# Attention with sparsemax on one core: small queries on column tiles, a head loaded from two queues, split relus in the last batch, and a new order

## The chip, the core and the metric

The kernel runs on one core of a Trainium2 chip. The core has a matrix engine (TensorE, PE), which multiplies a stationary block of up to 128x128 by moving columns and writes into PSUM; three engines for elementwise work (VectorE or DVE, ScalarE or ACT, GpSimd or POOL); and SyncE (SP), used here as a queue that issues transfers between main memory and on-chip memory (SBUF). Each engine executes its own instructions in order and waits for the others by semaphores. The metric is the device time of one launch in microseconds (us), as the median of several runs. A profiled execution is one run with a hardware trace.

## The reference

Eight batches of 100 rows with 512 features go through a cross-attention block with 16 heads of 32 features and a two-branch feed-forward block, all in 32-bit floats. The context of each batch has 722 rows.

```python
qh = split_heads(layernorm(x) @ Wq + bq)
kh = split_heads(ctx @ Wk + bk)
vh = split_heads(ctx @ Wv + bv)
scores = einsum('bhqd,bhkd->bhqk', qh, kh) * 32 ** -0.5
attn = sparsemax(scores)              # max(s - tau, 0), tau so that each row sums to 1
x = x + merge_heads(attn @ vh) @ Wo + bo
h = layernorm(x)
real = h @ cos(theta + theta_noise)
imag = h @ sin(phi + phi_noise)
out = x + sqrt(real ** 2 + imag ** 2)
```

Sparsemax needs a threshold tau for each row of scores. It is the fixed point of an iteration over the largest scores of the row.

## The kernel before

**Tiles.** The 800 rows of x are laid end to end and cut into seven token tiles: six of 128 rows and, fourth in order, a small one of 32 rows (`TILES`, with `HD` = 32). Layer norm, queries, output product and feed-forward go by token tile; keys, scores, sparsemax, values and weights go by batch. The context comes transposed, so that a chunk of 128 features lies on the 128 partitions.

**Scores and thresholds.** For each batch the 100 queries of the 16 heads give 13 groups of 128 score rows. Five *fills* (`fill`, L800, L789) write scores into the one large PSUM tile `psc` of four banks, by matmuls with 32 rows of contraction that share the array. ACT copies each fill to SBUF (`fill_copy`, L811), and DVE takes the eight largest of each of 24 segments of a row (`tops`, L822). From these `rests` and `candidates` make a list of 80 candidates in a row. `first_bound` gives a first threshold, and five rounds improve it (`above` on DVE, `above_values` on POOL, `above_count` and `update` on DVE). `losses` (three DVE instructions, L985 to L987) finds the largest score that may have been left out of the list; `keep_checks` on POOL keeps it for a verdict at the end, after which a slower path is taken if the list was too short. `parts` on POOL splits the thresholds into three bf16 parts, `parts_T` transposes them on PE (L951). In the last batch the thresholds are made in three spans of the groups (5, 4 and 4 of them), so that the first are done sooner.

**Weights and outputs.** A second set of matmuls makes the scores again, now transposed and less the threshold (`weights`, L995 and L1008), five pairs of a head group and a context chunk at a time, again in `psc`. A relu with the scale moves them to SBUF (`weights_relu`, L1027 on ACT), and `outputs` (L1042) multiplies them with the values. In the last batch the relus of odd number write into a buffer of the fills (`s_t`), the others into `aT`; the last of the five is cut in two, heads 0 and 1 on ACT (L1027) and heads 2 and 3 on DVE (L1029).

**Queries.** `queries` (L554) makes the four groups of 128 query features one after the other: `Wq` is stationary, the normed rows, transposed, are moving. For the small tile there are 32 moving columns. `small_product` (L580), used for the small tile's other three products, makes the rows stationary instead and writes the four groups of 128 features under each other, 32 partitions each, so that the four column tiles of the array work side by side.

**Head.** DVE fills a bf16 tile with -1, and PE multiplies it with itself `WARM` times (`warm_up`, L512) before the first real work. The first batch's keys are made by chunks of features as these land: `load_pair` issues a chunk of `Wk` (256 KB) and of the context (361 KB) on SP's queue, and `keys_part` (L706) multiplies six pieces (three head groups, two halves of the context).

**Tail.** The last token tile is finished by `last_steps_of_all`: its output product goes in four parts as the head groups come in, its feed-forward in two halves of 352 and 160 columns (`half_ffn`, L638, then `half_square`, `half_sum`, `half_root`, `half_result`), each half with its own store.

**The order.** Every step is a task with an engine, a cost in us (`STEPS`), the tasks it needs, and the buffers it takes (`hold`). `Plan.order` simulates the engines: an engine that is free takes the task that can start first, and among these the one with the earliest due time. The due time comes from the batch (`PERIOD`, `SHIFT`), the longest path to the end, and a table of shifts for each kind of step and batch (`LAG`, `NUDGE`); on PE a task whose use of the array is the same as that of the one before (`SHAPE`: full, 32x32, column tiles, row tiles) counts as `STAY` us earlier. The tasks are then emitted in the order of their simulated starts, and that is the order of the instructions on every engine and queue. `SHAPE` and `CHANGE` also give a cost in the plan for each change of the array's use. `LATENCY` is the plan's delay from one engine to the next.

Of the kernel before, what the change touches and what calls it, by code (L numbers as in the profile page):

```python
# [11 lines left out]
FP = mybir.dt.float32  # L12
# [9 lines left out]
HD = 32  # L22
# [24 lines left out]
def fills_of(left_first):  # L47
# [34 lines left out]
WARM = 32  # L82
# [17 lines left out]
    "load x": ("SP", 0.7),  # L100
# [3 lines left out]
    "load bias": ("SP", 0.1),  # L104
    "load pair": ("SP", 1.9),
    "warm up": ("PE", 2.1),
    "stats": ("DVE", 0.85),
    "deviation": ("ACT", 0.25),
    "normed": ("DVE", 0.72),
# [30 lines left out]
    "values last": ("PE", 2.7),  # L140
# [10 lines left out]
    "small residual": ("DVE", 0.9),  # L151
# [14 lines left out]
    "half result": ("DVE", 0.15, 0.00105),  # L166
    "store": ("SP", 0.6),
# [10 lines left out]
SHAPE = {"fill": 1, "fill last": 2, "outputs": 2, "small product": 2, "values last": 2, "weights": 3}  # L178
CHANGE = (0.19, 0.1, 0.1, 0.1)
STAY = 70.0  # L180

SHIFT = (-195.0, -175.0, -45.0, -130.0, -190.0, -205.0, -190.0, -220.0)
PERIOD = 121.0
WINDOW = 0.0
LAG = {
    "above": -95.0,
    "above count": -140.0,
    "above values": 280.0,
    "add bo": 265.0,
    "bounded": -170.0,  # L190
    "candidates": 295.0,
    "checks": 170.0,
    "deviation": -255.0,
    "ffn": 300.0,
    "fill": -290.0,
    "fill copy": -95.0,
    "fill last": -220.0,
    "first bound": -65.0,
    "half ffn": 230.0,
    "half result": 285.0,  # L200
    "half root": -130.0,
    "half square": -155.0,
    "half sum": -40.0,
    "keys": 115.0,
    "keys bias": 10.0,
    "keys part": -215.0,
    "leftovers": -85.0,
    "load bias": 85.0,
    "load ctx": 215.0,
    "load pair": -270.0,  # L210
    "load w": -80.0,
    "load x": -285.0,
    "load x again": 185.0,
    "losses": 75.0,
    "normed": -200.0,
    "normed 2": -120.0,
    "normed T": -145.0,
    "normed copy": 175.0,
    "output product": -10.0,
    "outputs bias": -85.0,  # L220
    "parts": -75.0,
    "parts T": 160.0,
    "parts copy": -300.0,
    "parts copy last": -200.0,
    "product part": -120.0,
    "queries": -300.0,
    "queries bias": -125.0,
    "relu ACT": 155.0,
    "relu DVE": 300.0,
    "residual": -85.0,  # L230
    "rests": -140.0,
    "result": -210.0,
    "sines": 230.0,
    "small product": -250.0,
    "small residual": -130.0,
    "small root": 55.0,
    "small square": -245.0,
    "small sum": -275.0,
    "square": -240.0,
    "square sum": -10.0,  # L240
    "stats": 290.0,
    "stats 2": 290.0,
    "store": -285.0,
    "tops": 175.0,
    "turned": 175.0,
    "turns": -70.0,
    "update": -85.0,
    "values": 210.0,
    "values copy": -205.0,
    "values last": 260.0,  # L250
    "values last copy": 220.0,
    "verdict": 155.0,
    "verdict T": 220.0,
    "verdict most": 90.0,
    "warm up": -60.0,
    "weights": -110.0,
    "weights relu": 265.0,
# [3 lines left out]
    "deviation": {6: 45.0},  # L261
    "ffn": {2: 150.0, 5: 150.0},
    "fill": {7: 190.0},
    "fill last": {2: -85.0},
    "first bound": {7: 150.0},
    "keys": {1: 10.0, 7: -100.0},
    "load bias": {0: 15.0},
    "load pair": {0: 35.0},
    "load w": {0: 170.0},
    "load x": {0: 50.0, 3: -20.0, 4: -180.0},  # L270
    "normed T": {2: 30.0},
    "output product": {2: 200.0},
    "outputs": {6: 20.0, 7: -25.0},
    "product part": {7: 110.0},
    "values": {0: 5.0, 2: -130.0, 3: -125.0, 5: -20.0, 6: 30.0, 7: 120.0},
    "weights": {1: 105.0, 5: 140.0, 6: 130.0},
# [16 lines left out]
class Plan:  # L293
# [3 lines left out]
    LATENCY = {"PE": 0.25, "SP": 2.0}  # L297
# [43 lines left out]
    def order(self):  # L341
# [8 lines left out]
        while len(done) < len(self.tasks):  # L350
            best = None
            for engine, waiting in ready.items():
                now, pick = free_at[engine], None
                for t in waiting:
                    start = max([now, t.ready] + [self.slot(h["name"]) for h in t.takes])
                    if start < math.inf:
                        stay = STAY if engine == "PE" and t.shape == shape else 0.0
                        key = (max(start, now + WINDOW), t.due - stay)
                        if pick is None or key < pick[0]:
                            pick = (key, start, t)  # L360
# [19 lines left out]
            for n in t.next:  # L380
                late = self.LATENCY.get(t.engine, 0.2)
                n.ready = max(n.ready, t.end + (0.0 if n.engine == t.engine == "SP" else late))
# [7 lines left out]
def xattn_ffn(  # L390
# [55 lines left out]
    def load_x(rows_of_x, n):  # L446

        x_t = rows.tile([P, DM], FP, name="x_t", bufs=3)[:n]
        nc.sync.dma_start(x_t, rows_of_x)
        return x_t  # L450
# [5 lines left out]

    def load_pair(st, b, c):

        if c == 0:
            st["c"] = big.tile([P, NG, S], FP, name="c_t")  # L460
# [126 lines left out]

    def small_residual(tk):
# [72 lines left out]
    def half_result(tk, h):  # L661
        a = tk["sq", 0][:, half_of(h)]
        nc.vector.tensor_tensor(a, a, tk["x"][:, half_of(h)], ALU.add)
# [32 lines left out]
    def keys_part(st, c):  # L696
# [7 lines left out]
        for n in range(EARLY):  # L704
            g, i = divmod(n, 2)
# [370 lines left out]
    def once(fn):  # L1076
        return add("load bias", fn)

    def set_x(tk):
        at, n = tk["at"], tk["n"]  # L1080
        tk["x"] = load_x(x.rearrange("b q d -> (b q) d")[at : at + n], n)
# [27 lines left out]
    def token_steps(tk):  # L1109
# [3 lines left out]
        hold("x", tk["x in"], [h])  # L1113
# [508 lines left out]
```

## Time and profile before

| What | Value |
|---|---|
| Median of three runs | 591.64 us (591.42 to 594.48) |
| Profiled execution, its own time | 594.34 us |
| Its span, first to last instruction | 592.6 us |
| Mean granted clock of PE | 0.995 |
| First matmul of the warm-up | 1.19 us |
| First matmul of the keys | 4.79 us |
| First `tops` on DVE | 30.07 us |
| Last group of half products begins | 585.68 us |
| Last store issued | 588.39 us |
| POOL busy | 224.2 us (38%) |
| Bytes moved by transfers | 26.61 MB |

A row of a profile gives the engine, the line of the kernel, the operation, the tile that is written and what is read, the shape, and the count. A matmul in 32-bit floats is two instructions. Matmuls overlap in the array, so their own durations are longer than the distance from one start to the next. The line of waits names an engine, what it was about to do, and which instruction of which engine ended the wait. A view by stretches gives each engine's busy time between two times, and the share of PE's clock that was granted.

### The profile page before, as it was taken

What the parts mean: (1) busy time and instruction counts of PE and PEld (TensorE: products, weight loads), DVE (VectorE), ACT (ScalarE), POOL (GpSimd) and SP (SyncE); (2) the same over time, 40 slices, a digit from 0 to 9 for tenths busy, and PEclk for the clock granted to TensorE, in tenths of its full rate; (3) what the DMA queues carried; (4) which work ended last, traced back from release to release, by engine and by line L of the source; (5) the groups of instructions that cost most, each with busy time, mean ns of one, the idle gap of its engine ahead of it and who ended that gap; (6) DMA issues with size and microseconds to landing.
All of it is one profiled execution on the core that took longest, in us unless ns stands there. A gap on an engine that the chain in (4) does not pass through costs nothing.

```text
span 592.6 us, 18085 instructions
## 1 busy us (share of the span) xinstructions
PE 580.5 (98%) x6937; PEld 339.1 (57%) x6937; DVE 517.3 (87%) x3186; ACT 261.8 (44%) x399; POOL 224.2 (38%) x293
## 2 busy tenths in 40 slices
PE   9999999999999999999999999999999999999995
PEld 6655554567456743677457744576557544664553
DVE  3299999998999879998999899999999899999521
ACT  1353352455346523654345434363545534552532
POOL 1686799974400232004620232015200446045402
PEclk9999999999999989999999999999999999999999
DMA  8940300310011000200100002030000001000001
GB/s 323 316 136 20 118 19 19 108 49 2 19 35 70 2 1 2 102 3 20 43 2 3 2 2 101 3 102 2 3 2 2 14 25 59 3 20 1 3 2 39
DMA packets 12475, 26.61 MB, mean 45 GB/s; under 512 B 1872, under 2 KB 2128, under 8 KB 12384
## 3 DMA queue, kind: packets, MB, share of 16 engines
q1 hardware_dynamic: 11952, 24.03, 12.4%
q8 instruction: 56, 0.92, 0.6%
q0 software_dynamic: 432, 1.38, 0.6%
q14 instruction: 35, 0.29, 0.2%
HBM read 23.76 MB, written 1.64 MB: 43 GB/s over the span
## 4 chain that ended last, share of the span: by engine, by line
PE 60%; DVE 32%; POOL 4%; ACT 2%; issue 1%; DVEq 0%; POOLq 0%; ACTq 0%
PE pm L717 18%; DVE cand L822 15%; PE pm L738 10%; PE psc L1008 5%; PE pm L612 5%; PE pm L1042 4%; PE psc L800 4%; PE pm L554 3%; DVE f L907 3%; DVE m L889 3%; POOL p L894 2%; DVE n L900 2%; PE pm L754 2%; PE psc L706 2%; PE psc L995 2%; DVE rest L831 1%
## 5 line engine op out<-in xcount | busy, mean ns | idle before, releaser
L822 DVE MAX8 cand<-s_t 128x8 f32<-128x30 f32 x2496 | 230.7, 171 | 1.4 <-ACT s_t L811 1.4
L894 POOL TENSOR_TENSOR p<-z,m 128x1040 f32<-128x1040 f32 (+2 forms) x50 | 88.7, 1778 | 266.7 <-DVE m L889 261.8
L717 PE MATMUL pm<-c_t,wk_sb 128*128 128x361 f32 x464 | 152.5, 474 | 0.0
L738 PE MATMUL pm<-wv_sb,c_t 128*128 128x512 f32 x320 | 144.3, 598 | 0.0
L717 PEld LDWEIGHTS pm<-c_t,wk_sb 128*128 128x128 f32 x464 | 84.1, 189 | 53.8 <-issue 10.8
L738 PEld LDWEIGHTS pm<-wv_sb,c_t 128*128 128x128 f32 x320 | 58.5, 190 | 66.7 <-issue 65.6
L811 ACT COPY s_t<-psc 128x1924 f32<-128x1924 f32 (+2 forms) x40 | 69.1, 1726 | 50.1 <-DVE cand L822 30.0
L1027 ACT ACTIVATE aT<-psc 128x2000 f32<-128x2000 f32 (+2 forms) x38 | 66.5, 1749 | 53.2 <-PE pm L1042 36.2
L767 ACT COPY v_t<-pm 128x512 f32<-128x512 f32 x40 | 23.4, 586 | 85.1 <-PE pm L738 85.1
L907 DVE TENSOR_REDUCE f<-p 128x13 f32<-128x1040 f32 (+2 forms) x50 | 50.4, 1009 | 10.6 <-POOL p L894 10.5
L728 ACT ACTIVATE k_t<-pm,bk_sb 128x361 f32<-128x361 f32 x60 | 33.5, 562 | 55.8 <-PE pm L717 55.7
L900 DVE TENSOR_REDUCE n<-m 128x13 f32<-128x1040 bf16 (+2 forms) x50 | 50.3, 1007 | 0.6
L1008 PE MATMUL psc<-q_t,k_t 32*128 32x100 f32 (+1 forms) x1536 | 47.4, 264 | 0.0
L1008 PEld LDWEIGHTS psc<-q_t,k_t 32*128 32x128 f32 (+1 forms) x1536 | 46.4, 180 | 0.4
L800 PE MATMUL psc<-k_t,q_t 32*32 32x481 f32 (+1 forms) x1536 | 43.3, 474 | 0.8 <-ACT s_t L811 0.7
L1042 PE MATMUL pm<-aT,v_t 128*32 128x100 f32 (+1 forms) x1440 | 39.2, 251 | 0.1
L1042 PEld LDWEIGHTS pm<-aT,v_t 128*32 128x32 f32 (+1 forms) x1440 | 30.9, 109 | 7.1 <-issue 3.3
L554 PEld LDWEIGHTS pm<-hT,wq_sb 128*128 128x128 f32 x224 | 27.1, 191 | 6.3 <-issue 5.4
L554 PE MATMUL pm<-hT,wq_sb 128*128 128x128 f32 (+1 forms) x224 | 29.6, 280 | 0.0
L800 PEld LDWEIGHTS psc<-k_t,q_t 32*32 32x32 f32 x1536 | 14.0, 103 | 26.2 <-issue 19.4
L754 PE MATMUL pm<-wv_sb,c_t 128*18 128x128 f32 (+1 forms) x384 | 23.6, 311 | 0.0
L831 DVE MAX8 rest<-cand 128x8 f32<-128x120 f32 x104 | 20.1, 268 | 0.2
(307 smaller groups left out, 615.6 us busy)
## 6 DMA issues: line engine op xcount, KB each, us to landing
c_t<-in_ctx SPq DMA_DIRECT2D x7, 1444.0 KB, 6.6
x_t<-in_x SPq DMA_DIRECT2D x12, 256.0 KB, 3.1
c_t<-in_ctx SPq DMA_DIRECT2D x4, 361.0 KB, 5.1
out<-sq POOLq DMA_DIRECT2D x5, 256.0 KB, 2.8
wk_sb<-in_L_xattn_Wk SPq DMA_DIRECT2D x4, 256.0 KB, 4.6
wq_sb<-in_L_xattn_Wq SPq DMA_DIRECT2D x4, 256.0 KB, 5.7
cos_sb<-in_L_ffn_theta SPq DMA_DIRECT2D x4, 256.0 KB, 4.5
n_t<-in_L_ffn_theta_noise SPq DMA_DIRECT2D x4, 256.0 KB, 3.1
```

The costliest lines, as they stand in the source:

```text
L554: nc.tensor.matmul(tk["pq"][:, g, : tk["n"]], lhsT=wq_sb[:, c, g * P : (g + 1) * P], rhs=tk["hT"][:, c, :], start=(c == 0), stop=(c == NG ...
L717: nc.tensor.matmul(pk, lhsT=wk_sb[:, c, g * P : (g + 1) * P], rhs=st["c"][:, c, i * SH : (i + 1) * SH], start=(c == 0), stop=(c == NG - 1),)
L738: nc.tensor.matmul(pv, lhsT=st["c"][:, k, c * CK : (c + 1) * CK], rhs=wv_sb[:, k, :], start=(k == 0), stop=(k == NG - 1),)
L800: nc.tensor.matmul(psc[b * HD : (b + 1) * HD, j, at : at + EDGE[hi] - EDGE[lo]], lhsT=st["q"][r, g, qb * HD : (qb + 1) * HD], rhs=st["k"][ ...
L811: nc.scalar.copy(s_t[:, :, :n], st["psc"][:, :, :n])
L822: nc.vector.max(st["cand"][:, n, k, :], st["s", f][:, j, at + EDGE[k] - first : at + EDGE[k + 1] - first],)
L894: nc.gpsimd.tensor_tensor(st["p"][:, lo:hi], st["z"][:, lo:hi], st["m"][:, lo:hi], ALU.mult)
L900: nc.vector.tensor_reduce(n_t, st["m"][:, lo:hi], AX.X, ALU.add)
L907: nc.vector.tensor_reduce(s_t, st["p"][:, lo:hi], AX.X, ALU.add)
L1008: nc.tensor.matmul(psc[:m, j, k * Q : (k + 1) * Q], lhsT=st["k"][r, g, lo : lo + m], rhs=st["q"][r, g, :], start=False, stop=(k == len(PAI ...
L1027: nc.scalar.activation(a, b, AF.Relu, scale=SCALE)
L1042: nc.tensor.matmul(st["po", g][j * HD : (j + 1) * HD, :Q], lhsT=st["v"][:m, c, f : f + HD], rhs=aT[j][:m, j, k * Q : (k + 1) * Q], start=( ...
```

## The change

1. `WARM` goes from 32 to 20.
2. The first chunk of the first batch's keys is loaded in two steps (`load_first`): `Wk`'s first 128 columns and then the other 384 on ACT's queue, the two halves of the context on SP's. `keys_part` goes through the first half of the context for all three head groups and then through the second.
3. The small tile's queries are made by `small_product`, copied from PSUM into the small tile's own buffer of x (`small_copy`, on ACT) and transposed on PE (`small_T`), after which the bias is added as before. The buffer of x is held until the transpose.
4. In the last batch all five relus are cut in two: heads 0 and 1 on ACT, heads 2 and 3 on DVE, with the buffers `aT` and `s_t` changing sides from one to the next.
5. `losses` is put ahead of the last (or only) `first_bound` of a batch, which now waits for it.
6. The second half of the last result is added on POOL instead of DVE.
7. In the plan, tiled work after tiled work of another kind counts as `STAY_TILED` us earlier; some costs and the delay after SP are changed; and the tables of shifts are new, so that the whole program has another order.

```diff
-WARM = 32
+WARM = 20
@@ STEPS
-    "load x": ("SP", 0.7),
+    "load x": ("SP", 0.85),
-    "load bias": ("SP", 0.1),
+    "load bias": ("SP", 0.45),
+    "load bv": ("SP", 0.45),
+    "load bo": ("SP", 0.8),
+    "load first": ("SP", 1.3),
-    "warm up": ("PE", 2.1),
+    "warm up": ("PE", 2.3),
-    "normed": ("DVE", 0.72),
+    "normed": ("DVE", 0.9),
+    "small queries": ("PE", 0.95),
+    "small copy": ("ACT", 0.33),
+    "small T": ("PE", 0.15),
+    "last result": ("POOL", 0.1, 0.0026),
...
-STAY = 70.0
+STAY = 155.0
+STAY_TILED = 140.0
-PERIOD = 121.0
+PERIOD = 147.0
...
-    LATENCY = {"PE": 0.25, "SP": 2.0}
+    LATENCY = {"PE": 0.25, "SP": 2.6}
...
-                        stay = STAY if engine == "PE" and t.shape == shape else 0.0
+                        stay = 0.0
+                        if engine == "PE":
+                            stay = STAY if t.shape == shape else STAY_TILED if t.shape and shape else 0.0
...
-                late = self.LATENCY.get(t.engine, 0.2)
-                n.ready = max(n.ready, t.end + (0.0 if n.engine == t.engine == "SP" else late))
+                late = 0.0 if n.engine == t.engine else self.LATENCY.get(t.engine, 0.2)
+                n.ready = max(n.ready, t.end + late)
...
+    def load_first(st, b):
+        st["c"] = big.tile([P, NG, S], FP, name="c_t")
+        for i in range(2):
+            w_cols = slice(P, DM) if i else slice(0, P)
+            nc.scalar.dma_start(wk_sb[:, 0, w_cols], wk[:P, w_cols])
+            keys_i = slice(i * SH, (i + 1) * SH)
+            nc.sync.dma_start(st["c"][:, 0, keys_i], ctxT[b, :P, keys_i])
...
+    def small_copy(tk):
+        tk["qs"] = tk["x whole"][:, :P]
+        nc.scalar.copy(tk["qs"], tk["pq"])
+    def small_T(tk):
+        pt = ps1.tile([P, NG, P], FP, name="pm")
+        nc.tensor.transpose(pt[:, 0, :], tk["qs"], ident)
+        tk["pq"] = pt[:, 0, :].rearrange("p (g t) -> p g t", g=NG)
...
-    def half_result(tk, h):
+    def half_result(tk, h, engine):
         a = tk["sq", 0][:, half_of(h)]
-        nc.vector.tensor_tensor(a, a, tk["x"][:, half_of(h)], ALU.add)
+        engine.tensor_tensor(a, a, tk["x"][:, half_of(h)], ALU.add)
...
-        for n in range(EARLY):
-            g, i = divmod(n, 2)
+        for i, g in sorted((n % 2, n // 2) for n in range(EARLY)):
...
+        if tk["n"] == HD:
+            pq = add("small queries", lambda: small_product(tk, "pq", "hT", wq_sb), hT, *w["q"])
+            cp = add("small copy", lambda: small_copy(tk), pq)
+            qs = [add("small T", lambda: small_T(tk), cp)]
+            hold("hT", hT_in, [pq])
+            hold("pm", pq, [cp])
+            hold("x", tk["x in"], qs)
...
-            rz = add("half result", lambda h=h: half_result(tk, h), rt, tiles=z - a)
+            rz = add(
+                "last result" if h else "half result",
+                lambda h=h: half_result(tk, h, nc.gpsimd if h else nc.vector), rt, tiles=z - a,
+            )
...
+            if hi == NT:
+                ls = add("losses", lambda st=st: losses(st), *cds, *rest_steps)
+            t = add(
+                "first bound", lambda st=st, r=r: first_bound(st, **r), cd, *([ls] if hi == NT else ()),
+                tiles=hi - lo,
+            )
...
-        ls = add("losses", lambda st=st: losses(st), *cds, *rest_steps)
...
-            if b == B - 1 and n == len(PAIRS) - 1:
+            if b == B - 1:
                 es = [
                     add(
                         "relu ACT" if k else "relu DVE",
                         lambda st=st, n=n, k=k: weights_relu(
-                            st, n, not k, slice(0, 2) if k else slice(2, HG), k
+                            st, n, (n + k) % 2 == 0, slice(0, 2) if k else slice(2, HG), k
                         ),
-                        f, tiles=len(pairs),
+                        f, *top_steps, tiles=len(pairs),
                     )
-                    for k in (True, False)
+                    for k in (1, 0)
                 ]
-                takes = {"aT": es[0], "s": es[1]}
+                takes = {"aT": es[n % 2], "s": es[1 - n % 2]}
```

## The prediction

> **What bounds the kernel now.** I read the busy times first, then the stretches of the run, then the waits of the matrix engine, then the order in time at three places.
>
> ```profile
> PE 580.5 (98%) x6937; PEld 339.1 (57%) x6937; DVE 517.3 (87%) x3186; ACT 261.8 (44%) x399; POOL 224.2 (38%) x293
> ```
>
> TensorE (PE) is in use in all but 12.1 us of the 592.6 us span. The five stretches show where VectorE (DVE) comes close.
>
> ```profile
> 0.00:30.00 30.00, 28.81 (x165) 20.07 (x166) 8.65 (x33) 8.19 (x16) 12.27 (x26) 1.00 0.92 317
> 30.00:165.00 135.00, 134.17 (x1414) 74.99 (x1413) 129.17 (x813) 57.62 (x81) 99.69 (x114) 1.00 0.17 54
> 165.00:464.00 299.00, 298.88 (x3920) 178.06 (x3919) 284.06 (x1846) 140.91 (x206) 65.51 (x84) 0.99 0.08 25
> 464.00:545.00 81.00, 80.05 (x940) 42.04 (x940) 78.32 (x444) 37.85 (x64) 35.34 (x44) 1.00 0.07 22
> 545.00:592.60 47.60, 38.58 (x501) 23.92 (x501) 17.12 (x54) 17.25 (x34) 11.40 (x28) 0.98 0.04 14
> ```
>
> The columns after the length are the busy time of PE, weight loads, DVE, ACT and POOL, then the granted clock. Between 30 and 545 us PE idles 1.9 us and DVE 23.4 us (5.83, 14.94 and 2.68 in the three stretches). So the time is PE's work, plus its few waits, plus a head and a tail; DVE stands right behind with 23 us of air in 515. What shortens PE's work counts in full as long as DVE can follow.
>
> PE's waits in the tail, from the waits of the last 52 us and the order in time:
>
> ```profile
> PE pm L1042 <- ACT s_t L1027: 1.2, 1, 1.2
> PE pm L951 <- POOL t L944: 1.1, 1, 1.1
> PE psc L995 <- ACT s_t L1027: 1.0, 1, 1.0
> ```
>
> Two of them (1.16 and 0.97 us) wait for a relu of 1.84 us on ACT between the weights and what needs their one PSUM tile. Further waits are 0.70 at 94.75 and 0.68 before the last half products.
>
> **The profiled execution and the median.** It took 594.34 us (span 592.6 and 1.74 around it), the median is 591.64. Part of the 2.70 between them is a clock window:
>
> ```profile
> 204.84:208.25 3.41, 3.41 (x56) 3.22 (x56) 2.55 (x4) 2.20 (x5) 2.17 (x1) 1.00 0.00 0
> 208.25:211.66 3.41, 3.41 (x6) 1.35 (x6) 3.24 (x6) 0.00 (x0) 0.72 (x1) 0.50 0.00 0
> ```
>
> For 3.41 us PE had half its clock, and eight 512-column matmuls took 5.21 us in place of 3.43: 1.78 us. The window before it holds the small tile's queries (L554, 32 columns a matmul). The Trainium skill ("TensorE: Matmul & The Clock Gate", Part 1) says the clock falls after an idle window of about 3.4 us; here PE was busy in all 3.41 us, so the row goes further than the rule: thin work was enough. By the rule nothing is owed to the queries; by the row the change also spares 1.78 us in executions that meet this. The runs (591.42, 591.64, 594.48) look like two without and one with it, so my sum for the median takes no credit, and 1.78 only on the profiled execution: 594.34 - 1.78 = 592.56, and 0.92 stays unexplained.
>
> **The change, part by part.**
>
> *Small tile's queries.*
>
> ```profile
> 204.46 1.97 PE L554 MATMUL pm<-hT,wq_sb 128*128 128x32 f32 x16
> 206.36 0.90 PE L1042 MATMUL pm<-aT,v_t 128*32 128x100 f32 x32
> 207.19 1.08 PE L554 MATMUL pm<-hT,wq_sb 128*128 128x32 f32 x8
> ```
>
> Sixteen took 1.90 us from start to next start, so all 32 some 3.6 (0.112 each, the pace of weight loads). On column tiles the same count is done as in L580: there 32 matmuls of 128x128 follow each other in 0.90 to 1.01 us. Added: one transpose (0.11 to 0.2) and a copy on ACT (0.33, hidden, ACT is 44% busy, though the queries' bias comes some 0.8 us later; its batch is filled 50 us later). Shape changes: a full-array group after a tiled one takes 2.63 us where the same group after its like takes 2.43, so 0.19 to come back and about 0.1 to leave; the old queries, cut in pieces between outputs, paid that too. Net **-2.4** (-2.1 to -3.0).
>
> *Head.* Warm-up ends at 4.79 (32 times 0.107 from 1.19) and the keys start at once, at half clock: 0.60 us per 361 columns until 6.86, then 0.30. With 20 matmuls it ends at 3.33. The first 250 KB, which is now all that the first matmul needs (64 KB of Wk, 185 of context), had moved by 3.02, the old first pair (617 KB) by 3.96. ACT's queue begins with a table load (0.87 to 2.15) that may hold its two issues, then 3.7 is likelier. Started at 3.6, PE does 3.26 us at half clock until 6.86 in place of 2.07: half of the difference is the gain, **-0.6**. The Trainium skill ("DMA: Bandwidth & Descriptors", Issuing engines are not separate DMA queues) speaks against more: two queues share the same engines and save issue time alone; the trace agrees, 0.42 us per issue on SP and 306 to 350 GB/s already. The clock page also warns that the warm-up is a time, not a count: should a gap after a shorter one cost a further window at half clock, it is +1.7 instead. SP's other loads keep their bytes; bo, bv and bq are needed later than their landing. Range -0.8 to +1.1.
>
> *Split relus.* Meant: 1.84 on ACT becomes 1.0 on ACT beside 1.22 on DVE (0.84 and 0.99 for 800 columns, scaled to 1000); up to -1.7 on the two waits above. But the one batch part already split does not run side by side:
>
> ```profile
> 570.32 0.99 DVE L1029 TENSOR_SCALAR s_t<-psc 128x800 f32<-128x800 f32 x1 [11.41 <-PE psc L1008]
> 571.41 0.84 ACT L1027 ACTIVATE aT<-psc 128x800 f32<-128x800 f32 x1 [2.21 <-DVE s_t L1029]
> ```
>
> ACT, idle for 2.2 us, starts when DVE has ended, 1.92 us in all where one ACT relu of 1600 columns would be about 1.5. If this holds for the four new splits, each is 1.22 + 0.1 + 1.0 = 2.3 us: +0.5 each, and since the order is made with 1.22, up to 1.1 each of uncovered wait, +4.4 in all. What covers it is other PE work between weights and outputs (values 3.6, ffn products 3.6): in the old order two of four places had such cover. So +1.0 with the old cover; I take **+0.5**, between -1.7 and +4.4, nearest to the measured pair. On DVE the halves add 4.9 us after 545, where it is busy 17.1 of 47.6; queued behind one is only the third part's Newton loop, which is used 8 us after it ends.
>
> *Losses ahead of the last first bound.* 0.71 + 0.18 + 0.17 = 1.06 us of DVE in each batch, only moved. In the last batch it leaves 551.98 (cover behind it: 8 us) and goes ahead of the third part's bound, near 531.8, where POOL's parts for the first transpose are waited for already (1.1). Some of it comes through: **+0.2** (0 to +1.06). It frees the candidates' buffer earlier, no more.
>
> *Last result on POOL.* 160 columns: 0.33 on DVE; on POOL 0.45 for 128 and 0.83 for 320, so 0.52. On the path of the last store: **+0.2**.
>
> *New order.* No row shows it. PE changes array shape 215 times (counted in the trace), 84 times back to the full array, some 29 us. The bonus for staying goes from 70 to 155, and tiled after tiled gets 140. Saving one return in fourteen is 6 x 0.19 = **-1.2** (-2.5 to +1.5). Waits of PE outside the relus: 1.1 + 0.7 + 0.7 + 0.4 = 2.9; a third of it, **-1.2** (-2 to +8, since a new order can also starve PE or DVE).
>
> Sum: -2.4 - 0.6 + 0.5 + 0.2 + 0.2 - 1.2 - 1.2 = -4.5. Median 591.64 - 4.5 = **587.1**; a profiled execution like the old one 594.34 - 1.78 - 4.5 = 588.1.
>
> **Rivals.** *Relus in series, uncovered* (the split doesn't do what it says): +4.4 in place of +0.5 gives 591.0, within 0.5%. For it: the ACT line above. Against it: values and ffn products that can lie between. *Relus side by side*: -1.7 in place of +0.5, 584.9; against it the same line. *Late fills starve DVE*, the slower end: the larger bonus keeps PE on full-array groups while a fill is due; DVE has two copies of a fill in hand (5.9 us each), so a fill that is over one keys group late (2.6 us) leaves it idle. The DVE account reads 30 + 491.6 busy + 23.4 idle + 47.6 = 592.6. Each late fill adds 2.6 to the idle; some 12 of the 14.9 us in the middle stretch are air in which DVE can catch up. So the time passes the old one from seven late fills on ((4.5 + 12) / 2.6 = 6.3), of 40, and eight give 587.1 + 20.8 - 12 = 595.9. For it: DVE is the chain that ends last from 30 to 165 and from 464 to 545; against it: only 2.7 us of its old idle lie in the last of these.
>
> **How the numbers follow.** About 0.5% (3 us) is what a measurement here can tell from no change: under 588.7 is faster, over 594.6 slower. Forecast 0.56 (own range 584.5 to 588.7), side by side 0.12 (faster too), series uncovered 0.19, starved 0.13. Faster 0.68, same 0.19, slower 0.13. The range leaves out half the starved case and the best of the side-by-side one: 583.0 to 593.5.
>
> **What would show it.** Right: no L554 of 32 columns, 32 matmuls at L580 for the queries in about 1 us, no half-clock window near 205; first keys at 3.3 to 3.8; ACT's and DVE's halves one after the other, yet PE's relu waits under 2.6 in all; fewer than 215 shape changes. Wrong: DVE idle above 26 us between its first candidates and the last bound; a second cold window in the head; waits of PE at L1042 or L995 over 3 us.

## The result, and the profile after

The changed kernel takes **598.39 us** (median of 7 runs, 595.48 to 600.26); the kernel before, run beside it, 591.92 us (7 runs). The ratio is 1.0099, with a 95% interval of 1.0072 to 1.0127: about 1% slower, where 587.1 had been forecast. The profiled execution took 599.58 us, of which the span is 597.7; it is longer than that of before by 5.1 us of span.

The busy times, from the page of the changed kernel:

```profile
PE 578.6 (97%) x6926; PEld 336.6 (56%) x6926; DVE 520.3 (87%) x3189; ACT 257.9 (43%) x400; POOL 225.0 (38%) x294
```

PE is busy for 1.9 us less and yet the span grew, so PE's idle time grew from 12.1 to 19.1 us. The chain that ended last changed its main engine; in the page of before it was PE with 60% and DVE with 32%:

```profile
DVE 49%; PE 37%; issue 6%; POOL 5%; DMA 1%; ACT 1%; SPq 0%; POOLq 0%; DVEq 0%; ACTq 0%
```

The five stretches of the changed kernel (columns: busy time of PE, weight loads, DVE, ACT, POOL, then the granted clock):

```profile
0.00:30.00 30.00, 27.55 (x151) 18.52 (x152) 7.50 (x33) 7.68 (x15) 12.06 (x25) 1.00 0.94 328
30.00:165.00 135.00, 134.42 (x1394) 76.72 (x1392) 129.68 (x839) 59.98 (x82) 98.23 (x113) 1.00 0.14 45
165.00:464.00 299.00, 296.73 (x4010) 175.58 (x4010) 282.24 (x1822) 141.20 (x209) 69.05 (x85) 1.00 0.08 27
464.00:545.00 81.00, 76.31 (x798) 38.89 (x802) 78.01 (x441) 33.60 (x64) 35.19 (x47) 0.96 0.07 22
545.00:597.70 52.70, 43.61 (x579) 26.84 (x579) 22.86 (x58) 15.44 (x33) 10.44 (x25) 0.96 0.04 13
```

Between 464 and 545 us PE is busy for 76.31 us in place of 80.05, and the clock is 0.96: 3.7 of the 7.0 us of new idle time lie there, and the lost clock beside them. (Another 1.3 lie in the first 30 us and 2.2 between 165 and 464.) The longest of PE's waits from 464 us to the end:

```profile
PE pm L989 <- POOL t L982: 2.8, 1, 2.8
PE pm L651 <- ACT hT L573: 1.4, 1, 1.4
PE psc L1033 <- DVE aT L1067: 1.2, 1, 1.2
PE psc L1033 <- ACT aT L1065: 1.1, 1, 1.1
```

The first two are new. They begin at 517 and 507 us, and PE's clock falls to half within the later one, at 518.86. Stretches of 3.41 us there, the length for which the kernel before had half its clock, in the changed kernel:

```profile
515.45:518.86 3.41, 1.49 (x44) 1.31 (x43) 3.34 (x29) 2.79 (x4) 1.42 (x4) 1.00 0.02 5
518.86:522.27 3.41, 2.19 (x5) 1.17 (x6) 3.41 (x39) 1.32 (x6) 2.38 (x7) 0.50 0.01 2
522.27:525.68 3.41, 3.41 (x6) 1.34 (x5) 3.20 (x18) 0.37 (x3) 1.55 (x2) 0.50 0.20 77
```

The reason for the waits shows on DVE, 40 us earlier. The order in time of DVE, then of POOL, in the changed kernel:

```profile
473.10 0.09 DVE L557 RECIPROCAL rs<-sd 32x1 f32<-32x1 f32 x1
473.30 4.07 DVE L559 TENSOR_SCALAR h_t<-x_t,mv,rs 32x512 f32<-32x512 f32 x1
477.30 2.64 DVE L860 MAX8 cand<-s_t 128x8 f32<-128x30 f32 x28
```

```profile
473.08 0.59 POOL L723 DMA_DIRECT2D out<-sq  x1 [0.31 <-POOL sq L722]
473.69 2.17 POOL L932 TENSOR_TENSOR p<-z,m 128x1040 f32<-128x1040 f32 x1
475.81 1.28 POOL L577 TENSOR_TENSOR x_t<-x_t,bo_sb 128x512 f32<-128x512 f32 x1
```

The small tile's second normalisation takes 0.53 us where POOL is idle (a run below). Here it takes 4.07 us and ends 0.28 us after three POOL instructions have run one behind the other, so DVE loses 3.5 us. In the kernel before the same step took 1.18 us, at 471.27. What follows can be read in the order in time. DVE's search for the last batch's candidates runs on without a gap and comes 3.5 us later. A fill of that batch, in its PSUM tile since 501.95, waits for DVE to free a buffer and is copied at 513.97 only; the weights of the batch before need that tile (515.79). The last batch's first transposes wait for POOL, which waits for DVE: 2.80 us, with the values queued behind them on PE. That this one instruction is the cause is so far a reading of one trace; the experiments test it.

Of the marks that the prediction set, these came true: the first keys at 3.81 us, the small queries as 32 column-tiled matmuls in 1.06 us at 206.07, no half clock near 205, relu waits of 2.3 us in all, 212 shape changes (counted as before). DVE's idle time between 30 and 545 us is 25.1 us, under the 26 that was to show starvation: DVE did not starve, it was stretched, and the stretched time counts as busy.

### The profile page after: what moved, and what is told of

The parts are those of the page before. It is cut to its first block, busy times and chain, and to the rows that moved or that the text cites. A ratio compares the mean times of both kernels' runs of the same rounds, so it can differ in the third digit from the quotient of the medians.

```text
span 597.7 us, 18080 instructions
## 1 busy us (share of the span) xinstructions
PE 578.6 (97%) x6926; PEld 336.6 (56%) x6926; DVE 520.3 (87%) x3189; ACT 257.9 (43%) x400; POOL 225.0 (38%) x294
## 3 DMA queue, kind: packets, MB, share of 16 engines
q0 software_dynamic: 432, 1.38, 0.6%
## 4 chain that ended last, share of the span: by engine, by line
DVE 49%; PE 37%; issue 6%; POOL 5%; DMA 1%; ACT 1%; SPq 0%; POOLq 0%; DVEq 0%; ACTq 0%
DVE cand L860 24%; PE pm L776 11%; PE pm L755 6%; DVE m L927 5%; DVE f L945 5%; DVE n L938 4%; PE psc L1046 3%; PE pm L1080 3%; PE pm L583 3%; POOL p L932 3%; PE pm L651 2%; PE psc L838 2%; DVE rest L869 2%; PE pm L792 1%; DVE t L895 1%
## 5 line engine op out<-in xcount | busy, mean ns | idle before, releaser
L755 PE MATMUL pm<-c_t,wk_sb 128*128 128x361 f32 x464 | 150.0, 473 | 0.0
L776 PE MATMUL pm<-wv_sb,c_t 128*128 128x512 f32 x320 | 147.9, 610 | 0.0
L1065 ACT ACTIVATE aT<-psc 128x2000 f32<-128x2000 f32 (+3 forms) x38 | 64.8, 1705 | 65.0 <-PE pm L1080 41.6
L1080 PE MATMUL pm<-aT,v_t 128*32 128x100 f32 (+1 forms) x1440 | 41.4, 251 | 0.0
L1080 PEld LDWEIGHTS pm<-aT,v_t 128*32 128x32 f32 (+1 forms) x1440 | 32.6, 109 | 7.2 <-issue 4.0
L583 PE MATMUL pm<-hT,wq_sb 128*128 128x128 f32 x192 | 22.8, 277 | 0.0
L583 PEld LDWEIGHTS pm<-hT,wq_sb 128*128 128x128 f32 x192 | 22.0, 192 | 1.1 <-issue 0.6
L547 DVE BATCH_NORM_STATS2 st<-x_t 128x6 f32<-128x512 f32 (+1 forms) x14 | 9.5, 679 | 12.8 <-DMA x_t<-in_x 12.6
```

The source lines that it names most:

```text
L583: nc.tensor.matmul(tk["pq"][:, g, : tk["n"]], lhsT=wq_sb[:, c, g * P : (g + 1) * P], rhs=tk["hT"][:, c, :], start=(c == 0), stop=(c == NG ...
L755: nc.tensor.matmul(pk, lhsT=wk_sb[:, c, g * P : (g + 1) * P], rhs=st["c"][:, c, i * SH : (i + 1) * SH], start=(c == 0), stop=(c == NG - 1),)
L776: nc.tensor.matmul(pv, lhsT=st["c"][:, k, c * CK : (c + 1) * CK], rhs=wv_sb[:, k, :], start=(k == 0), stop=(k == NG - 1),)
L1065: nc.scalar.activation(a, b, AF.Relu, scale=SCALE)
L1080: nc.tensor.matmul(st["po", g][j * HD : (j + 1) * HD, :Q], lhsT=st["v"][:m, c, f : f + HD], rhs=aT[j][:m, j, k * Q : (k + 1) * Q], start=( ...
```

## The experiments

To try edits without the new order, and the order without the edits, the plan's order is written out as a list in the kernel:

```diff
-        for t in plan.order():
-            t.emit()
+        for n in ORDER:
+            plan.tasks[n].emit()
```

Ratios below are to runs of the kernel before on the same chip (1.0099 for the changed kernel). "Ahead" compares the starts of the same group of matmuls in two traces.

**All edits, old order.** The five edits of the diff, with ORDER as the kernel before has it. The old order reuses the small tile's x tile early, so the small copy goes to a tile for leftover queries:

```diff
     def small_copy(tk):
-        tk["qs"] = tk["x whole"][:, :P]
+        tk["qs"] = ql[1].rearrange("p g t -> p (g t)")
         nc.scalar.copy(tk["qs"], tk["pq"])
...
         nc.tensor.transpose(pt[:, 0, :], tk["qs"], ident)
+        nc.gpsimd.memset(ql[1], 0.0)
```

> All five edits (small queries on column tiles, loads from two queues with 20 warm-up matmuls, split relus, losses ahead of the last first bound, last result on POOL) emitted in the order of the kernel before, written out as a list. The small queries' copy goes to a leftover-query tile that POOL zeroes again, since the old order already reuses the x tile. If the new order is what cost the time, the edits alone keep my terms -2.4 -0.6 +0.5 +0.4: about 589.5 us, 588 to 591. If the edits themselves cost it (relus in series with no cover, a stalled head), it is above 594.

Measured: 598.39 us, ratio 1.0092 (1.0070 to 1.0114). That is the second theory's number, though not its reasons: the edits cost time without the new order too, and the head is not stalled. That the median equals the changed kernel's is chance, as the causes differ. PE is 0.97 us ahead at the first keys, 1.12 at 213 us, 0.12 at the transposes at 545, and 4.0 behind at the last weights. The order in time of PE in this run:

```profile
545.38 0.28 PE L975 MATMUL pm<-ident_b,t 128*128 128x128 bf16 x2 [2.22 <-POOL t L968]
545.50 5.35 PE L762 MATMUL pm<-wv_sb,c_t 128*128 128x512 f32 x8
```

PE waits 2.22 us where the kernel before waited 1.14, and the values behind it take 5.35 us in place of 3.65: half clock, 1.7 us. A further 2.4 us go between the first and the last weights of the last batch, where the relus are. So the edits' cost here is the losses' and the relus', which the last two runs try one by one. The gain at 207 us was small in this run because I had queued the small copy on ACT ahead of a relu that PE needs (1.79 us of wait); that was my placing, not the edit.

**The order, no edits.** ORDER as the changed kernel has it, all steps as before.

> The steps of the kernel before, none of the edits, emitted in the order of the changed kernel. If the order is what cost the time: 598 to 602 us, with the waits of PE near 506 to 520 us there again. If the order is innocent and an edit is to blame: 592 or less.

Measured: 599.36 us, ratio 1.0105 (1.0079 to 1.0131). The order alone costs as much as the whole change, as the first theory had it. The same DVE instruction takes 4.07 us again (at 476.24), and the same two waits follow (1.38 and 2.79). Against this run the edits show their worth in the new order: the small queries put PE 2.6 us ahead at 207 us. The head's 0.88 at the first keys is gone by 10 us (0.1 behind). (The old queries stand in one piece here, thin work of 3.6 us, and some clock is lost behind them that the edit spares.)

**One DVE step moved.** The changed kernel; in ORDER one entry stands later, behind two `tops` and an `update`.

```diff
-normed 2 (small tile), tops, tops, update, above
+tops, tops, update, normed 2 (small tile), above
```

> The changed kernel in its own order, with one DVE step moved: the small tile's second normalisation (reciprocal and the 4.07 us tensor_scalar h_t) goes two steps later, to a place where POOL is idle. If that stretched instruction is what put DVE behind and so made PE wait at 506 to 520 us: the instruction takes 0.55 us, the waits fall from 4.6 us to 2 or less, and the time falls by 3 to 6 us, to 592.5 to 595.5. If DVE's lag is not what PE waited for, the time stays at 598.

Measured: 593.81 us, ratio 1.0019 (1.0006 to 1.0032): 4.6 us less for one instruction moved by some 4 us. It takes 0.53 us there, after POOL's three instructions, which end at 477.37 (DVE in order of time):

```profile
477.80 0.53 DVE L559 TENSOR_SCALAR h_t<-x_t,mv,rs 32x512 f32<-32x512 f32 x1
```

The wait for hT at 507 us is gone and the one for POOL falls from 2.8 to 1.6. The matmuls behind it have the full clock, so PE is 5.85 us ahead of the changed kernel at the next weights (526 us there): 3.1 from the waits, 2.8 from the clock.

**Relus unsplit, new order.** The changed kernel with the last batch's relus as before.

```diff
-            if b == B - 1:
+            if b == B - 1 and n == len(PAIRS) - 1:
...
             else:
+                spare = b == B - 1 and n % 2 == 1
...
```

> The changed kernel in its own order with the relus of the last batch as they were before (one engine for each of the first four, halves for the last). If the serial halves are what cost the time: at least 3 us faster than the changed kernel, 595 or less. If they are covered by PE's other work as my sum took them: within 1.5 us of the changed kernel, 597 to 600.

Measured: 597.61 us, ratio 1.0074 (1.0048 to 1.0100), 0.8 less than the changed kernel by the medians and 1.5 by the ratios, with intervals that overlap; in the trace PE gains 0.8 us by 526 us, where nothing was changed, and 0.5 from there to the last weights. The split costs little here.

**The two PE savings alone, old order.** From the diff, these parts and no others:

```diff
-WARM = 32
+WARM = 20
...
+            c_in.append(add("load first", lambda st=st, b=b: load_first(st, b)))
...
+            pq = add("small queries", lambda: small_product(tk, "pq", "hT", wq_sb), hT, *w["q"])
...
```

> Two edits only, in the order of the kernel before written out: small queries on column tiles, and the head (two queues, 20 warm-up matmuls). Relus, losses and last result as before. Both save PE work and add nothing to DVE. If PE's work counts in full, as my sum had it: -2.4 - 0.6, so 589.0. In the run of all five edits PE stood only 1.1 us ahead at 213 us and DVE's end held it back to 0.1 at 545 us; if what took that 1.0 back was the losses alone, 591.2 here, with PE 1.0 to 1.2 us ahead at the transpose near 545 us. If DVE's chain binds in any case, PE waits longer there and nothing is left: 592.3.

Measured: 592.89 us, ratio 0.9999 (0.9984 to 1.0013). PE was 1.24 us ahead at 213 us and stayed so to the last weights, as the second reading had it; the median doesn't show it. The trace has the relu's wait of 1.8 us from my placing of the small copy, so the queries' saving was not yet measured.

**Losses alone, old order.** These lines of the diff; besides, the written-out order has the small tile's queries in one piece:

```diff
             cd = add("candidates", ...
+            if hi == NT:
+                ls = add("losses", lambda st=st: losses(st), *cds, *rest_steps)
             t = add("first bound", ...
...
-        ls = add("losses", lambda st=st: losses(st), *cds, *rest_steps)
```

> One edit only, in the order of the kernel before: losses (three DVE instructions, 1.06 us) ahead of the last first bound in every batch. My sum gave it +0.2. If DVE's chain sets the transpose near 545 us, all 1.06 us come through there: PE's wait for POOL's parts grows from 1.14 to about 2.2 us and the time by 1.0, to 593.4; a wait of over 2 us can also be followed by half clock, as in the run of all five edits (1.7 us more). If it is covered: 592.5.

Measured: 595.21 us, ratio 1.0047 (1.0029 to 1.0064), 2.8 us for 1.06 us of DVE work that was only moved. PE in order of time:

```profile
549.08 0.28 PE L958 MATMUL pm<-ident_b,t 128*128 128x128 bf16 x2 [2.21 <-POOL t L951]
549.20 5.35 PE L745 MATMUL pm<-wv_sb,c_t 128*128 128x512 f32 x8
```

The wait grew by 1.07, all of the moved work, and half clock came with it (1.7 us). But behind the 32 thin queries in one piece PE had half clock too and stood 2.6 us behind at 217 us. So the 2.8 were not yet the losses' own; the last run below has them on another base.

**The small tile's normalisation on ACT, new order.** The step stays in its place, on another engine:

```diff
+        if tk["n"] == HD and "py" in tk:
+            mean = tk["mv"][:, 0:1]
+            nc.scalar.activation(mean, mean, AF.Identity, scale=rs)
+            nc.scalar.activation(tk["h"], tk["x"], AF.Identity, bias=mean, scale=rs)
+            return
         nc.vector.tensor_scalar(
```

with the mean's sign turned beside the deviation.

> The changed kernel in its own order, with the small tile's second normalisation computed on ACT (x * rs - mean * rs) in its old place, in place of the 4.07 us tensor_scalar on DVE. If POOL's instructions kept that DVE instruction from starting: the time falls as with the moved one, to 593 to 594.5, and no DVE instruction near 473 us is over twice its usual length. If something else held DVE at 473 to 477 us, the next DVE instructions are stretched in its place and the time stays near 598.

Measured: 592.75 us, ratio 1.0006 (0.9991 to 1.0021): 5.6 us less than the changed kernel, and no longer to be told from the kernel before. DVE goes from the reciprocal straight on, while POOL does the same three instructions at 473.19 to 477.20 (DVE, then PE, in order of time):

```profile
473.21 0.09 DVE L560 RECIPROCAL rs<-sd 32x1 f32<-32x1 f32 x1
473.23 2.63 DVE L868 MAX8 cand<-s_t 128x8 f32<-128x30 f32 x28
```

```profile
516.25 0.28 PE L997 MATMUL pm<-ident_b,t 128*128 128x128 bf16 x2 [1.34 <-POOL t L990]
516.37 3.65 PE L784 MATMUL pm<-wv_sb,c_t 128*128 128x512 f32 x8
```

So it was not the place in DVE's queue but that instruction beside POOL's work. The Trainium skill ("SBUF — State Buffer", Who interferes with whom) names a reason: a tensor_scalar in a two-port mode takes the port pair that DVE shares with GpSimd, as a lock for the whole instruction. No view shows the mode or the lock. But the traces agree with one: all ten normalisations that are stretched in the two kernels, before and changed, end 0.28 us after the end of a POOL instruction that ran beside them, and POOL's three took the same 4.01 us with the DVE instruction beside them and without it.

**Old order, two normalisations moved.** In the kernel before, seven of the 14 normalisations are stretched. Five are of 128 rows: 2.40 us at 155.19, 1.12 at 219.45, 1.23 at 290.16, 2.41 at 347.46, 1.63 at 488.75, in place of 0.55. Two are the small tile's, 1.22 at 88.42 and 1.18 at 471.27, and were left alone, though a later expectation speaks of five in all. The first of them with what POOL did (DVE, then POOL, in order of time):

```profile
155.19 2.40 DVE L530 TENSOR_SCALAR h_t<-x_t,mv,rs 128x512 f32<-128x512 f32 x1
```

```profile
155.16 2.15 POOL L894 TENSOR_TENSOR p<-z,m 128x1040 f32<-128x1040 f32 x1 [2.02 <-DVE rs L528]
157.27 1.46 POOL L548 TENSOR_TENSOR x_t<-x_t,bo_sb 128x512 f32<-128x512 f32 x1
```

The first and the last of the five were moved in DVE's queue:

```diff
-normed, above count, tops, update
+above count, tops, update, normed
...
-normed 2, above
+above, normed 2
```

> As the run of the two PE savings in the old order, and two normalisations moved in DVE's queue away from POOL's work: the one at 155.19 us (2.40 us in place of 0.55) behind the next update, the one at 488.75 us (1.63) behind the next 'above'. Aimed at beating both kernels. If DVE's chain is what binds at 155 and at 545 us: 1 us more than the PE savings alone bring, 590.0 to 590.5, and the wait of 1.14 near 545 us shrinks. If DVE's lag does not matter there: the same as the PE savings alone.

Measured: 591.40 us, ratio 0.9985 (0.9973 to 0.9996), 1.5 us under the run without the moves, somewhat more than expected; the level stands 1 us higher, since the relu's wait of 1.79 us is still in it. The first now takes 0.55 us, the last still 1.24, and the wait near 545 us did not shrink (1.15).

**The new order, mended.** The normalisation on ACT, the relus unsplit, and the first tile's transposes behind the second keys part on PE:

```diff
-keys part 0, normed T, keys part 1
+keys part 0, keys part 1, normed T
```

> The changed kernel in its own order with three things mended: the small tile's second normalisation on ACT (as in the run before), the first transposes of the normalised tile behind the second keys part instead of ahead of it (PE waited 0.95 us there for DVE at 10.2 us), and the relus of the last batch unsplit. If these three are what separates the changed kernel from its sum: 592.7 - 0.9 - 0.8 = 591.0. If PE's waits come back elsewhere because DVE's chain follows behind: 592.5.

Measured: 592.03 us, ratio 0.9990 (0.9977 to 1.0003): 0.7 us less, not 1.7. In the trace it is 0.85: the relus brought 0.5, and of the head's 0.9 there were 0.4 left at the third keys part, since the next wait stood behind the removed one. The longest of PE's waits in the first 30 us:

```profile
PE psc L737 <- DMA c_t<-in_ctx: 1.7, 1, 1.7
```

In the new order SP loads bo, the first x and two biases ahead of the second pair of ctx and Wk, and the second and third keys parts wait for those pairs.

**The PE savings, mended.** As the run of the two PE savings, with the small copy behind the relu on ACT:

```diff
-small copy, weights relu
+weights relu, small copy
```

> The two PE savings (small queries, head) in the old order once more, with the small tile's copy on ACT put behind the relu of the same moment instead of ahead of it: in the run before, that relu waited for the copy and PE 1.79 us for the relu, which was my placing and not the edit. If the queries save what my sum said: PE 2.5 to 3.0 us ahead at 215 us, and if DVE lets it through, 590.0 to 590.7. If DVE's chain takes it back before 545 us: PE ahead at 215 us but no more than 1 us at 545, time 591.5.

Measured: 591.63 us, ratio 0.9981 (0.9971 to 0.9991). PE is 4.7 us ahead of the kernel before at 214 us, of which 1.8 is the half-clock window that the kernel before has there and this run doesn't: 2.9 from the edits, as the sum had it. Then 1.2 go again at the next weights. PE in order of time:

```profile
243.75 0.39 PE L1019 MATMUL psc<-tT,neg_b 3*128 3x500 bf16 x4 [0.94 <-ACT s_t L835]
```

PE waits for a fill's copy, which waits for a buffer that DVE has still to search. DVE does take it back, before 245 us and not, as I had expected, towards 545.

**Old order, all five moved.**

The three further moves, in DVE's queue:

```diff
-normed 2, above count, tops
+above count, tops, normed 2
...
-normed, above count
+above count, normed
...
-normed 2, above count, tops, update
+above count, tops, update, normed 2
```

> As the run of the PE savings mended, and all five normalisations that POOL stretched in the kernel before (2.40, 1.12, 1.23, 2.41 and 1.63 us in place of 0.55) moved in DVE's queue to places where POOL is idle. If DVE's lag is what takes PE's lead back: 1 to 1.5 us under the run without the moves, 589 to 589.7. If DVE has air there: the same as without the moves.

Measured: **590.05 us**, ratio 0.9957 (0.9944 to 0.9970), 1.6 us under the run without the moves and faster than both kernels. The wait at 243 us is gone: PE is 5.1 us ahead of the kernel before at 214 us and 4.9 at the end (1.8 of it that kernel's half-clock window). Of the five instructions one is still stretched (1.23 us at 484.68). Not separated by these runs: each move shortens an instruction, and also lets the steps of the threshold's rounds go ahead of it.

**Split relus added to it.** The diff's part for the last batch, each half where the ACT relu stood:

```diff
-            if b == B - 1 and n == len(PAIRS) - 1:
+            if b == B - 1:
                 es = [
...
```

> The fastest run so far (old order, two PE savings, five moves) with the split relus of the last batch added, each DVE half queued where the ACT relu stood. The run of all five edits lost some 2.4 us between the first and the last weights of the last batch, but with a half-clock window beside it. If the halves run one after the other, ACT's 1.0 and DVE's 1.2 us, and nothing new covers them: PE's waits for relus grow from 2.9 to 4.5 us or more, and the time is 1.5 to 3 us over the run without them, 591.5 to 593. If the cover is there, as my sum took it with +0.5: 590.5. If they ran side by side: 588.5.

Measured: 592.44 us, ratio 1.0007 (0.9999 to 1.0015): the split costs 2.4 us in this order by the medians, 3.0 by the ratios, and 2.3 between the first and the last weights of the last batch in the traces. The halves run in turn (ACT, then DVE, in order of time):

```profile
564.24 1.00 ACT L1051 ACTIVATE s_t<-psc 128x1000 f32<-128x1000 f32 x1 [0.90 <-PE psc L1032]
```

```profile
565.27 1.20 DVE L1053 TENSOR_SCALAR aT<-psc 128x1000 f32<-128x1000 f32 x1 [4.74 <-ACT s_t L1051]
```

That is 2.23 us in place of the 1.84 of one ACT relu; DVE's half waits for ACT's, and why it does no run here tells. The size is as the first reading had it, the place is not. PE's relu waits in the tail are no longer than before (1.7 against 2.1 in the run without the split). What grew is its wait for POOL's parts, from 1.1 to 3.0 us in three places: DVE waits 1.2 us for ACT's half at 547.3 and only then goes on with the third part's Newton steps.

**Losses added to it.** The lines of the run of the losses alone, without the split relus:

```diff
+            if hi == NT:
+                ls = add("losses", lambda st=st: losses(st), *cds, *rest_steps)
...
```

> The fastest run so far (old order, two PE savings, five moves) with the losses ahead of the last first bound added. In the earlier run with the losses alone the small tile's 32 thin query matmuls stood in one piece, and PE's clock fell behind them, so its 2.8 us may hold more than the losses; here the queries are on column tiles. If the moved 1.06 us of DVE work come through: PE's wait at the last batch's first transposes grows from 1.1 to about 2.2 us, and the time is 1.1 us over the run without it, 591.1, or 592.8 where half clock follows that wait as it did twice before. If DVE, relieved by the five moves, has the air to take it: 590.1.

Measured: 592.82 us, ratio 0.9994 (0.9981 to 1.0006), by the ratios 2.2 us over the run without them (2.8 by the medians). PE in order of time:

```profile
545.23 0.28 PE L975 MATMUL pm<-ident_b,t 128*128 128x128 bf16 x2 [2.21 <-POOL t L968]
545.35 5.35 PE L762 MATMUL pm<-wv_sb,c_t 128*128 128x512 f32 x8
```

Wait and half clock are the same as twice before: 1.07 and 1.7 us on the wait of 1.14 that the kernel before has there. So a move of 1.06 us costs over 2 us in this order, by trace and by ratio. The size is less sure than the place: this profiled execution began 3.2 us late with the second keys part, which waited for ctx (11.1 us against 7.9 in the run without the losses, with the same loads in the same order), and the kernel's runs spread from 590.08 to 596.24. Still the parts close the first experiment's sum: 592.89 for the two PE savings with the copy as it was placed there, 2.4 for the relus and 2.2 to 2.8 for the losses make 597.5 to 598.1, where all edits together took 598.39.

## Why the prediction was wrong, point by point

**New order, waits: the step that failed.** It was put at -1.2, "a third of it", with a far end of +8 "since a new order can also starve PE or DVE". It is the far end that came. The one stretched instruction costs 5.6 us (from 598.39 to 592.75): 3.5 on DVE, which reach PE as waits, and half clock with them (2.8 in the profiled execution; the mean clock of six of the seven runs was 0.991 to 0.994). I had looked for a rate in the waits of the old order, and a rate says nothing about a single coincidence of two engines. It was to be suspected: the trace of before has the same instruction at 1.12 to 2.41 us seven times beside POOL's work, and my account of DVE has no word on it. Nor is it the amount: against 0.55 us each, the seven lose 7.3 us on DVE in the kernel before, and in the changed kernel three lose 4.1. What counted was where the 3.5 fell, ahead of the last batch's thresholds, which PE waits for.

**The rival on the slower side** gave 596 and a mechanism, late fills and an idle DVE, that the traces refute: DVE's idle time rose by 1.7 us only. Right was its ground, that DVE is as close to the bound as PE. The opening statement that PE's work "counts in full as long as DVE can follow" was used as if the condition held. In the old order, 1.2 of the savings went back within 40 us, and came back when the five normalisations were moved.

**The rest of the gap.** Without the stall, at 592.75, 5.7 us are missing to 587.1. Between the trace of before and that of the run with the normalisation on ACT, PE's busy time fell from 578.7 (580.5 less the 1.78 of its clock window) to 575.9, by 2.8, where queries and shape changes were to save 3.6; its idle time grew from 12.1 to 14.9, where waits and relus were to make it 0.7 less. That is 0.8 and 3.5. Of the 2.8 of new idle time, 0.9 lie in the first 30 us and 2.2 between 165 and 464, where the kernel before had almost none; there PE waits for copies of fills (1.6 us at two weights, 0.9 at a fill). Which part of the new order brings them no run tried. Together they are 4.3 of the 5.7. Of the 1.4 that are left, 0.9 is what the prediction had left unexplained between its trace (592.56 without the clock window) and its median; 0.5 stays open.

**Shape changes**, -1.2 for six returns to the full array: 84 became 80, so -0.8. Counted by the tile shapes in the traces, the edits in the old order save one return, so most of it is the order's.

**Small queries**, -2.4: right. PE is 2.6 us ahead in the new order, 2.9 with the head in the old one, once the copy on ACT stands where no relu waits for it. (The 3.6 us put on the 32 old ones do not follow from 1.90 for sixteen, which makes 3.8; in one piece they take 3.59 in the run of the order alone.)

**Head**, -0.6: the start came as foreseen (3.81, 0.98 earlier), and in the new order nothing was left of it 6 us later. I had let "SP's other loads keep their bytes" stand for their order: bo, x and the biases went ahead of the second pair, and the first transposes ahead of the second keys part. In the old order the second keys part began anywhere from 7.9 to 11.1 us in seven profiled executions with this head (9.5 before), so that term has a spread of its own that no part of my sum held.

**Split relus**, +0.5 with ends of -1.7 and +4.4: 0.5 in the new order, in two traces, and 2.4 in the old. The reading of the one pair that was already split was right, halves in series, and so was the cover in the new order. What I had named as used "8 us after it ends", the Newton steps queued behind DVE's half, is what carries the 2.4 in the old order.

**Losses ahead**, +0.2 between 0 and 1.06: it depends on the order as well. In the old one all 1.06 came through, and half clock with it (2.2 by the ratios). In the new one the transposes that it could delay waited 0.17 us in the run with the normalisation on ACT, so there it seems covered; no run in the new order took the losses back.

**Last result on POOL**, +0.2: the instruction takes 0.51 us in place of 0.33, as put; its effect on the time was not tried by itself.

## What to carry to other kernels

Where two engines stand close to the bound, look up each instruction of the second one that has a wide spread between its shortest and longest time, and what the other engines did at that moment: a stretched instruction counts as busy, so neither busy shares nor idle times show it. Moving five small instructions in one queue brought 1.6 us of 590, and one such instruction in the wrong place cost 5.6, though the stretched time of these instructions had become less in all. An edit that only moves work is to be costed by what waits behind its new place, in the order in which it will run: head, relus and losses each cost one thing in the one order and another in the other.

## What was not expected of the hardware

A DVE tensor_scalar of 32x512 took 4.07 us in place of 0.53, to the hundredth the same in the three kernels that have it at that place (changed, order alone, relus unsplit), and two POOL instructions that began after it were done before it. The Trainium skill ("SBUF — State Buffer", Who interferes with whom) has the one that issues first take the shared ports; by that DVE should have gone ahead of those two. It is not always so. At 155.19 us in the kernel before, DVE ended at 157.59, with the first of two POOL instructions over at 157.31, and the second took 1.46 us in place of 1.28. What differs at 473 us is that POOL issues a transfer first; no run separates that. On ACT the same step left both engines' other times as they were.

Half clock came after waits shorter than 3.41 us: behind a wait of 2.2 us in three kernels (5.35 us in place of 3.65 for eight matmuls) and behind one of 1.79 in two kernels of three, but not behind one of 1.99 in the run of the losses added. So it is not the length of the wait alone. In each trace the changes of the clock lie on a grid of 3.41 us, and what fits is how much of the wait falls into one step of it. Two steps and the ones behind them, in the run of all edits and in that of the losses added (columns as above):

```profile
205.03:208.44 3.41, 1.62 (x39) 1.18 (x36) 2.58 (x3) 2.55 (x6) 2.36 (x2) 1.00 0.00 0
208.44:211.86 3.42, 3.42 (x6) 1.34 (x5) 3.21 (x7) 0.00 (x0) 1.24 (x1) 0.50 0.00 0
```

```profile
95.72:99.13 3.41, 1.58 (x34) 0.56 (x35) 3.38 (x19) 2.70 (x3) 3.24 (x4) 1.00 0.03 7
99.13:102.54 3.41, 3.41 (x9) 1.50 (x8) 3.41 (x34) 0.22 (x1) 3.24 (x3) 1.00 0.00 0
```

In the 15 traces, from the first full clock to the last 8 us, half clock followed all six full-clock steps with PE busy for 1.49 us or less, and two of the three around 1.6 (1.62 and 1.63, not 1.58). It followed none with 1.8 us or more, except three filled by the thin queries in full (3.41 of 3.41). In the run of two moves the wait of 1.79 us is shared by two steps, busy for 2.61 and 2.43, and nothing follows. The Trainium skill ("TensorE: Matmul & The Clock Gate", Part 1) speaks of an idle window of about 3.4 us; here a partly busy one was enough. A wait of PE of about 1.8 us or more can thus cost 1.7 us beyond its own length, by where it falls.
